# A graph layer on one core: half of the second messages behind the first factors, loads of h, gate weights and x re-timed, two last sums on GpSimd

## The chip, the cores and the metric

The kernel runs on one core of a Trainium2 chip. The metric is the device time of one launch in microseconds. The kernel before takes 1845.73 us, the median of three runs from 1843.53 to 1846.13 us. The profile was taken in a run of its own, whose span is 1848.1 us.

A core has five engines with instruction streams of their own: TensorE (PE in the profile; its weight loads are PEld), VectorE (DVE), ScalarE (ACT), GpSimd (POOL) and SyncE (SP). SP, ACT and GpSimd also issue transfers (DMA) between the memory outside the core and the core's own memory. "L597" is line 597 of the kernel before.

## The reference

There are 32 batches of 512 tokens with 256 channels. Each batch is normalised over its channels and cut at zero (h). From h come a convolution of 17 taps along the tokens, a message passing whose weights are distances between tokens, and a gate cell (a GRU step) that joins both.

```python
h = jnp.maximum(_layernorm(x, axis=-1), 0.0)
x = x + _L0_gnn_ref(h, adj, ...)

# _L0_gnn_ref, cut; here x is h and mask is adj
xc = jnp.transpose(x, (0, 2, 1))
h = _bn(_conv1d(xc, conv1_w, 0), ...)              # 1 tap
h = jax.nn.relu(h)
h = _bn(_conv1d(h, conv2_w, 8), ...)               # 17 taps
x_conv = jnp.transpose(jax.nn.relu(h + xc), (0, 2, 1))
s = x @ w_se.T + b_se                              # 3 numbers for each token
sq = jnp.sum(s * s, axis=-1)
dist = sq[:, :, None] + sq[:, None, :] - 2.0 * jnp.einsum('bnd,bmd->bnm', s, s)
A = jnp.exp(-dist) * mask
msg = jax.nn.relu(x @ w_msg.T + b_msg)
x_nmp = jnp.einsum('bnm,bmd->bnd', A, msg)
gi = jnp.concatenate([x_conv, x_nmp], axis=-1) @ w_ih.T + b_ih
gh = x @ w_hh.T + b_hh
r = jax.nn.sigmoid(gi_r + gh_r)
z = jax.nn.sigmoid(gi_z + gh_z)
nn_ = jnp.tanh(gi_n + r * gh_n)
return (1.0 - z) * nn_ + z * x
```

## The kernel before

The kernel works in three stages. The first two are done for half of the batches (16, called a group g) and then for the other half.

1. `first_part`: load x, normalise it, transpose it (h), do the convolution of 1 tap (`conv1`) and turn windows of its result into frequencies (`windows_to_freq`). For the second group GpSimd also builds sums of gate weights in this stage (`combine_weights`), one per turn of the loop over batches.
2. `nodes`: messages, distances and their product for each batch; between them stand the products of the 17-tap convolution in frequencies (`product`, tile `y`).
3. The gates for pairs of batches: the convolution's way back (`inverse`), `gates_rz`, `gate_n`, and `last_z` for the last pair.

The steps that the change touches, cut:

```python
def load_x(b, queue=nc.sync):
    X[b] = ... tile([P, NC, D], FP, tag="x", bufs=3)      # 512 KB
    queue.dma_start(X[b], x[b].rearrange("(c p) d -> p c d", p=P))

def statistics(b):
    for c in range(NC):
        nc.vector.bn_stats(stats[:, c, :], X[b][:, c, :])             # L285
    for c in range(NC):
        nc.vector.bn_aggr(mv[:, c, :], stats[:, c, :])                # L287
    ...
    nc.vector.tensor_scalar(rstd, mv[:, :, 1], LN_EPS, None, op0=ALU.add)            # L290
    nc.gpsimd.tensor_tensor(rstd, rstd, minus_half[:, :NC], op=ALU.pow)              # L291

# normalise(b): xn = (x - mean) * rstd on VectorE (L304)
# transpose_h(b): 8 transposes of xn on TensorE (phT), max with 0 on VectorE into hT (L316), hT stored to HD[b]
# conv1(b): 16 matmuls (pc), bias on VectorE (L331), relu on ACT

# first_part, the loop over the batches of a group (the turn of b0 itself cut):
for b in range(b0, b1):
    if b + 3 < b1:
        load_x(b + 3, nc.gpsimd)
    ...
    if b + 2 < b1:
        statistics(b + 2)
    if b + 1 < b1:
        transpose_h(b + 1)
    if b + 2 < b1:
        normalise(b + 2)
    one, two = between(b - b0)       # second group: one step of combine_weights
    if b > b0 + (g == 0):
        conv1(b)
    ...
    for step in one:
        step()
    windows_to_freq(b - 1, xf)

# combine_weights: for each of three weight matrices one load into a tile w (one buffer for w4),
# then four steps with one sum on GpSimd each (L886), and a store of the sums
if k == 0:
    steps.append([])
steps[-1].append(load)
...
    steps.append([partial(nc.gpsimd.tensor_tensor, q[dst], x1, x2, op=op)])

# by_chunks(b): ACT copies HT[b], in another order, to HQ[b] (L425)
def message(b):
    hq = HQ.pop(b)
    for c0 in range(0, NC, h):                     # two halves of two chunks
        for j in range(h):
            # 2 accumulating matmuls into a bank pm (L439), bias on VectorE: st (L441), msg (L442)
        nc.scalar.activation(m, m, AF.Relu)        # L443
# features(b): VectorE writes fl and fr from st
# factors(b): TensorE transposes fl (psl) and fr (psr), ACT copies them to sl (L460) and sr (L465)
# affinity(b): 4 matmuls pd of sl and sr (L474), exp on ACT, times adj on VectorE: A
# aggregate(b): matmuls pn of msg and A (L489), copied by ACT

# nodes(g, ...):
load_adj(todo[0])
begin(0)                                           # message and features of todo[0]
message(todo[1])
factors(todo[0])
features(todo[1])
affinity(todo[0])
for i, b in enumerate(todo):
    ...
    if i + 2 < GB and todo[i + 2] not in HT:
        load_h(todo[i + 2])                        # HD[b] back into hT, on the SP queue
    if more:
        load_adj(todo[i + 1])
        factors(todo[i + 1])
    ...                                            # a product, aggregate in parts
    begin(i + 2)                                   # by_chunks, message, features
    if more:
        affinity(todo[i + 1])
    ...

# last_z, the end of the kernel:
# turned(i, j): multiply and transpose on VectorE into o; added(i, j): xb += o on VectorE (L673)
turned(1, 0)
gated(b3, u3, 1, 1)                                # VectorE addition, sigmoid on ACT
nc.vector.tensor_add(u2, u2, b3)
added(1, 0)
store(p, 0, [nc.sync, nc.scalar])                  # four transfers, in turn on two queues
into(b5[0], ...); gated(b5[0], u2, 0, 1, ts[0])
turned(1, 1)
into(b5[1], ...); gated(b5[1], u2, 0, 1, ts[1])
added(1, 1)
for t in ts:
    turned(0, 1, t); added(0, 1, t); store(p, 1, [nc.sync, nc.scalar], t)
```

Of the kernel before, what the change touches and what calls it, by code (L numbers as in the profile page):

```python
# [11 lines left out]
FP = mybir.dt.float32  # L12
AF = mybir.ActivationFunctionType
ALU = mybir.AluOpType

P = 128
# [49 lines left out]
def gnn_layer(  # L66
# [15 lines left out]
    nc = tc.nc  # L82
    B, N, D = x.shape
    KT = w2T.shape[1]
    PAD = KT // 2
    NS = w_seT.shape[1]
# [338 lines left out]
            nc.scalar.copy(chunks(HQ[b][:, ic, :]), by_chunk(HT[b][:, ic, :]))  # L425
        del HT[b]

    def message(b):
        MSG[b] = pools["nodes"].tile([P, NC, D], FP, tag="msg", name=f"msg_{b}", bufs=3)
        ST[b] = pools["nodes"].tile([P, 2, NC, NS], FP, tag="st", name=f"st_{b}", bufs=2)  # L430
        hq = HQ.pop(b)
        h = N // D
        for c0 in range(0, NC, h):
            m = MSG[b][:, c0 : c0 + h, :]
            for j in range(h):
                c = c0 + j
                p = bank(f"pm_{b}_{c}")
                for ic in range(DC):
                    nc.tensor.matmul(p[:, : D + NS], hq[:, ic, c * P : (c + 1) * P], wmsg[:, ic, :],  # L439
                                     start=(ic == 0), stop=(ic == DC - 1))  # L440
                nc.vector.tensor_add(ST[b][:, 0, c, :], p[:, D : D + NS], bmsg[:, D:])  # L441
                nc.vector.tensor_add(m[:, j, :], p[:, :D], bmsg[:, :D])  # L442
            nc.scalar.activation(m, m, AF.Relu)  # L443

    def features(b):

# [62 lines left out]
    def combine_weights():  # L509

        steps = []
        for k, src in enumerate((w_hhT, w_ihT[D:], w_ihT[:D])):
            w, t = (pools["sums"].tile([P, n, 3 * P], FP, tag=f"w{n}", name=f"w{n}_{k}", bufs=m) for n, m in ((4, 1), (7, 2)))
            rows = w.rearrange("p (c h) m -> p c (h m)", c=DC)
            load = (partial(nc.sync.dma_start, rows, src.rearrange("(c p) m -> p c m", p=P)) if k == 1 else
                    partial(load_rows, rows, src, nc.sync))
            if k == 0:
                steps.append([])
            steps[-1].append(load)

            a11, a21, a12, a22 = (
                w[:, 2 * c : 2 * c + 2].rearrange("p h m -> p (h m)").rearrange("p (g i o) -> p g i o", i=2, o=32)[:, :, i]
                for c in range(DC) for i in range(2)
            )
            q = [t[:, n].rearrange("p (g o) -> p g o", o=32) for n in range(7)]
            for (dst, x1, x2, op), kept in zip(
                ((Q5, a21, a22, ALU.add), (Q6, q[Q5], a11, ALU.subtract),
                 (Q7, a11, a21, ALU.subtract), (Q3, a12, q[Q6], ALU.subtract)),
                ((Q1, a11), (Q2, a12), (Q4, a22), None),
            ):  # L530
                steps.append([partial(nc.gpsimd.tensor_tensor, q[dst], x1, x2, op=op)])
                if kept:
                    steps[-1].append(partial(nc.scalar.copy, q[kept[0]], kept[1]))
            steps[-1].append(partial(nc.sync.dma_start, WS[k], t.rearrange("p q (g o) -> p q g o", o=P)))
        return steps
# [58 lines left out]
    def into(bk, q, o, ks, terms, first, t=slice(0, N)):  # L594

        for i, k in enumerate(ks):
            nc.tensor.matmul(bk[:, t], sw[:, k, q, o, :], terms[k][q][:, t], start=(first and i == 0), stop=(i == len(ks) - 1),  # L597
                             skip_group_check=True)
# [50 lines left out]
    def last_z(p, terms):  # L649

        d, o, ks = RZ[p], 1, range(K3)

        def gated(src, other, i, j, t=slice(0, N)):
            z, g = d[:, DC + i, j, t], DC + i
            if other is not None:
                nc.vector.tensor_add(z, other[:, t], src[:, t])
                src = z
            nc.scalar.activation(z, src, AF.Sigmoid, bias=brz[:, g : g + 1], scale=1.0)

        def places(i, t):  # L660
            return slice(t.start // 32, t.stop // 32), slice(32 * i, 32 * (i + 1))

        def turned(i, j, t=slice(0, N)):
            dst, (js, half) = d[:, i, j, t], places(i, t)
            nc.vector.tensor_mul(dst, dst, d[:, DC + i, j, t])
            if (p, j) not in OUT:
                OUT[p, j] = pools["late"].tile([P, N // 32, D // 4], FP, tag="o", name=f"o_{p}_{j}", bufs=2)
            nc.vector.transpose(OUT[p, j][:, js, half], dst.rearrange("p (j k) -> p j k", k=32))

        def added(i, j, t=slice(0, N)):  # L670
            js, half = places(i, t)
            x = XP[p][j][:, js, half]
            nc.vector.tensor_add(x, x, OUT[p, j][:, js, half])  # L673

        b1, b2, b3, b4, *b5 = (bank(f"pz{k}_{p}") for k in range(1, 7))
        into(b1, Q1, o, ks, terms, True)
        p1 = temp("p1", f"z{p}")
        nc.scalar.copy(p1, b1)
        into(b2, Q6, o, ks, terms, True)
        u2 = temp("u2", f"z{p}")  # L680
        nc.vector.tensor_add(u2, p1, b2)
        into(b1, Q2, o, ks, terms, False)
        gated(b1, None, 0, 0)
        early_out(p, 1, 1)
        turned(0, 0)
        into(b2, Q7, o, ks, terms, False)
        u3 = temp("u3", f"z{p}")
        nc.vector.tensor_add(u3, p1, b2)
        early_out(p, 0, 1)
        added(0, 0)  # L690
        into(b4, Q4, o, ks, terms, True)
        gated(b4, u3, 1, 0)
        into(b3, Q5, o, ks, terms, True)
        turned(1, 0)
        gated(b3, u3, 1, 1)
        nc.vector.tensor_add(u2, u2, b3)
        added(1, 0)
        store(p, 0, [nc.sync, nc.scalar])

        ts = [slice(h * N // 2, (h + 1) * N // 2) for h in range(2)]  # L700
        into(b5[0], Q3, o, ks, terms, True, ts[0])
        gated(b5[0], u2, 0, 1, ts[0])
        turned(1, 1)
        into(b5[1], Q3, o, ks, terms, True, ts[1])
        gated(b5[1], u2, 0, 1, ts[1])
        added(1, 1)
        for t in ts:
            turned(0, 1, t)
            added(0, 1, t)
            store(p, 1, [nc.sync, nc.scalar], t)  # L710
# [90 lines left out]
    def store(p, j, queues, t=slice(0, N)):  # L801
        js = slice(t.start // 32, t.stop // 32)
        for g in range(4):
            queues[g % len(queues)].dma_start(quarter(out[2 * p + j], g)[:, js], XP[p][j][32 * g : 32 * (g + 1), js])
# [6 lines left out]
    def first_part(g, freq, between, left=()):  # L811
# [37 lines left out]
        normalise(b0 + 1, g > 0)  # L849
        fill()  # L850
        for b in range(b0, b1):
            if b + 3 < b1:
                load_x(b + 3, nc.gpsimd)
            if b == b0:
                conv1(b)
                one, two = between(0) if g == 0 else ([], [])
                for step in one:
                    step()
                fill()
                if g == 0:  # L860
# [3 lines that stand above are left out]
                else:  # L864
                    normalise(b + 2)
                    transpose_h(b + 1)
                fill()
                xf, last_two = freq(g), two
                continue
            if g == 0 and b == b0 + 1:  # L870
                conv1(b)
                for step in last_two:
                    step()
            if b + 2 < b1:
                statistics(b + 2)
            if b + 1 < b1:
                transpose_h(b + 1)
            if b + 2 < b1:
                normalise(b + 2)
            one, two = between(b - b0)  # L880
            if b > b0 + (g == 0):
                conv1(b)
            if b == b1 - 1:
                load_h(b0)
# [3 lines that stand above are left out]
            for step in two:  # L888
                step()
# [13 lines left out]
    with tc.tile_pool(name="freq", bufs=1) as fpool:  # L903
# [29 lines left out]
        def nodes(g, xf, units, last):  # L933
# [11 lines left out]
            load_adj(todo[0])  # L945
            with tc.manual_schedule():
                begin(0)
                message(todo[1])
                factors(todo[0])
                features(todo[1])  # L950
            affinity(todo[0])
            for i, b in enumerate(todo):
# [4 lines left out]
                    load_x(b1)  # L957
                if g + 1 < NG and i == 3 * GB // 4:
                    statistics(b1)
                if i + 2 < GB and todo[i + 2] not in HT:  # L960
                    load_h(todo[i + 2])
                if more:
                    load_adj(todo[i + 1])
                    factors(todo[i + 1])
# [4 lines left out]
                for u in mine[:1]:  # L969
                    product(pools["pw"], g, u, xf)  # L970
                begin(i + 2)
                if more:
                    affinity(todo[i + 1])
                for u in mine[1:2]:
# [109 lines left out]
```

## Time and profile before

| What | us |
|---|---|
| median of the runs | 1845.73 |
| span of the profile | 1848.1 |
| first part, first group | about 0 to 165 |
| nodes, first group | about 165 to 467 |
| first part, second group | about 467 to 580 |
| nodes, second group | about 580 to 880 |
| gates | about 880 to 1848 |
| TensorE busy | 1826.4 |
| VectorE, GpSimd, ACT busy | 1109.1, 588.2, 581.9 |

The limits of the stages are read from the chain of work that ended last, where the lines of one stage give way to those of the next.

How to read the answers of the profile that are shown below. A line of the view of waits names the engine, the tile and line that waited, what it waited for, and then the total in us, how often, and the longest. A line of the order of time gives the start in us, the length in us of the piece, engine, line and operation, the tile written and the tiles read, their shapes, the number of instructions merged, and in brackets the idle time before it and what ended that. A line of the view of windows gives the window, its length, the busy time of TensorE, of its weight loads, of VectorE, ACT and GpSimd (each with a count of instructions), then the granted clock of TensorE (1.00 is full), the share of the DMA engines, and GB/s.

### The profile page before, as it was taken

Reading aid. Unit: us, or ns where it says so; the run is one execution under the profiler, and the core shown is the slowest. Engines: PE = TensorE matmul, PEld = TensorE weight load, DVE = VectorE, ACT = ScalarE, POOL = GpSimd, SP = SyncE. Lnnn points to the kernel's source line nnn. Section 1 sums busy time; section 2 is a strip of 40 time slices with the busy share of each in tenths; the row PEclk is TensorE's granted clock in tenths of the full one; section 3 lists DMA queues with packets and bytes.
Section 4 is the critical chain, followed back from the end, with each engine's and each line's share of the span. In section 5 each row is a group of like instructions: output and inputs, shape, how many; then the busy total and the mean of one; then the engine's idle time right before and its main releaser. Section 6 shows DMA issues by size and latency. Waiting matters only on the chain.

```text
span 1848.1 us, 20105 instructions
## 1 busy us (share of the span) xinstructions
PE 1826.4 (99%) x6610; PEld 1089.0 (59%) x6610; DVE 1109.1 (60%) x2220; ACT 581.9 (31%) x1083; POOL 588.2 (32%) x572
## 2 busy tenths in 40 slices
PE   9999999999999999999999999999999999999998
PEld 6777666666888666665555554555455544555443
DVE  7775656554885555545266466655666466645666
ACT  4555434432335333333222221222122221222121
POOL 3331333333432344444422323133212322133221
PEclk9999999999999999999999999999999999999999
DMA  8999888875678887778421443234422442244312
GB/s 233 299 276 241 225 226 246 218 179 180 212 250 207 235 245 235 216 207 261 123 86 34 120 120 99 53 88 120 120 78 43 120 120 88 49 103 120 112 25 52
DMA packets 307452, 289.26 MB, mean 157 GB/s; under 512 B 148028, under 2 KB 237148, under 8 KB 306964
## 3 DMA queue, kind: packets, MB, share of 16 engines
q1 hardware_dynamic: 281300, 224.22, 46.0%
q10 hardware_dynamic: 19024, 38.68, 5.9%
q0 software_dynamic: 7024, 25.07, 4.8%
q8 instruction: 53, 0.87, 0.2%
q14 instruction: 51, 0.42, 0.1%
HBM read 191.50 MB, written 96.40 MB: 156 GB/s over the span
## 4 chain that ended last, share of the span: by engine, by line
PE 89%; DVE 4%; issue 3%; DMA 2%; POOL 1%; ACT 1%; SPq 0%; POOLq 0%; ACTq 0%; DVEq 0%
PE pg L597 29%; PE pn L597 14%; PE pn L489 11%; PE py L393 11%; PE pm L439 6%; PE pc L585 5%; PE pc L328 3%; PE px L343 3%; PE pw L256 2%; PE pd L474 2%; PE phT L312 1%; DMA w<-in_w_ihT_dram 1%; PE psr L463 1%; DVE stats L285 1%; DVE xn L304 1%
## 5 line engine op out<-in xcount | busy, mean ns | idle before, releaser
L489 PE MATMUL pn<-A,msg 128*128 128x512 f32 x512 | 225.9, 593 | 0.6 <-DVE A L480 0.6
L597 PE MATMUL pg<-hp,sw 128*128 128x512 f32 x434 | 221.8, 593 | 0.7 <-DVE rz L616 0.5
L597 PE MATMUL pg<-np,sw 128*128 128x512 f32 x434 | 221.6, 592 | 0.0
L597 PE MATMUL pg<-cp,sw 128*128 128x512 f32 x434 | 221.6, 592 | 0.0
L575 POOL TENSOR_TENSOR hp<-hp 128x512 f32<-128x512 f32 x64 | 81.3, 1280 | 413.0 <-DMA hp<-hd 234.6
L372 POOL TENSOR_TENSOR both<-xf 128x256 f32<-128x256 f32 x78 | 60.1, 771 | 329.1 <-PE py L393 297.5
L489 PEld LDWEIGHTS pn<-A,msg 128*128 128x128 f32 x512 | 97.2, 191 | 110.9 <-issue 105.7
L575 POOL TENSOR_TENSOR cp<-cp 128x512 f32<-128x512 f32 x64 | 80.4, 1267 | 229.8 <-ACT cp L591 228.6
L393 PE MATMUL py<-wt,both 128*128 128x256 f32 x624 | 151.0, 385 | 0.7 <-issue 0.7
L612 ACT ACTIVATE rz<-rz,brz 128x512 f32<-128x512 f32 x93 | 67.0, 721 | 260.2 <-DVE rz L616 260.2
L400 DVE TENSOR_TENSOR y<-y,py 128x256 f32<-128x256 f32 x78 | 31.8, 408 | 190.5 <-ACT y L399 185.8
L597 PEld LDWEIGHTS pg<-hp,sw 128*128 128x128 f32 x434 | 82.2, 190 | 104.8 <-issue 97.8
L597 PEld LDWEIGHTS pg<-cp,sw 128*128 128x128 f32 x434 | 82.5, 190 | 103.8 <-issue 103.8
L597 PEld LDWEIGHTS pg<-np,sw 128*128 128x128 f32 x434 | 82.5, 190 | 103.8 <-issue 103.8
L393 PEld LDWEIGHTS py<-wt,both 128*128 128x128 f32 x624 | 114.3, 190 | 43.2 <-issue 28.3
L480 DVE TENSOR_TENSOR A<-e,at 128x512 f32<-128x512 f32 x128 | 114.5, 933 | 36.9 <-ACT e L477 36.7
L359 POOL TENSOR_TENSOR wsum<-wt 128x512 f32<-128x512 f32 x78 | 109.1, 1399 | 51.8 <-DMA wt<-wd 39.1
L735 ACT ACTIVATE nt<-nt,vech 128x512 f32<-128x512 f32 x64 | 46.2, 722 | 235.8 <-DVE nt L734 235.8
L328 PE MATMUL pc<-w,hT 128*128 128x256 f32 x512 | 116.7, 381 | 1.6 <-DVE hT L316 1.6
L439 PE MATMUL pm<-wmsg,hq 128*128 128x259 f32 x512 | 117.5, 382 | 0.6 <-ACT sl L460 0.6
L597 PE MATMUL pn<-np,sw 128*128 128x512 f32 x224 | 114.4, 592 | 0.0
L597 PE MATMUL pn<-cp,sw 128*128 128x512 f32 x224 | 114.4, 592 | 0.0
(146 smaller groups left out, 2963.6 us busy)
## 6 DMA issues: line engine op xcount, KB each, us to landing
wt<-wd SPq DMA_DIRECT2D x160, 256.0 KB, 4.3
adj<-in_adj_dram SPq DMA_DIRECT2D x128, 256.0 KB, 5.4
wd<-wst SPq DMA_DIRECT2D x64, 320.0 KB, 5.3
yd<-y ACTq DMA_DIRECT2D x80, 256.0 KB, 4.3
yt<-yd SPq DMA_DIRECT2D x30, 640.0 KB, 7.5
hd<-hT SPq DMA_DIRECT2D x32, 512.0 KB, 4.4
nd<-nmp ACTq DMA_DIRECT2D x32, 512.0 KB, 4.0
xb<-in_x_dram SPq DMA_DIRECT2D x128, 128.0 KB, 3.8
```

The source lines that it names most:

```text
L328: nc.tensor.matmul(p[:, j, :], HT[b][:, ic, c * P : (c + 1) * P], w1[:, ic, :], start=(ic == 0), stop=(ic == DC - 1))
L343: nc.tensor.matmul(p[:, j * 2 * L : (j + 1) * 2 * L], H1[b][:, c0 + j, ic * P : (ic + 1) * P], fwd, start=True, stop=True)
L359: nc.gpsimd.tensor_tensor(t, WT[g, u][:, 0], WT[g, u][:, 1], op=ALU.add)
L372: nc.gpsimd.tensor_tensor(both[:, 0], re, im, op=ALU.add)
L393: nc.tensor.matmul(dst, v[:, ic, :], w[:, ic, :], start=(ic == 0), stop=(ic == DC - 1))
L439: nc.tensor.matmul(p[:, : D + NS], hq[:, ic, c * P : (c + 1) * P], wmsg[:, ic, :], start=(ic == 0), stop=(ic == DC - 1))
L480: nc.vector.tensor_mul(A[b][:, mc, :], e, at)
L489: nc.tensor.matmul(p, MSG[b][:, mc, dc * P : (dc + 1) * P], A[b][:, mc, :], start=(mc == 0), stop=(mc == NC - 1))
L575: nc.gpsimd.tensor_tensor(t[:, dst, :], t[:, a, :], t[:, b, :], op=sub)
L585: nc.tensor.matmul(bk[:, t0:t1], YT[p][j][:, c, oc * P : (oc + 1) * P], back[:, n : n + t1 - t0], start=(c == 0), stop=(c == len(spans) - ...
L597: nc.tensor.matmul(bk[:, t], sw[:, k, q, o, :], terms[k][q][:, t], start=(first and i == 0), stop=(i == len(ks) - 1), skip_group_check=True)
L612: nc.scalar.activation(rz[:, g, j, :], src, AF.Sigmoid, bias=brz[:, g : g + 1], scale=1.0)
```

## The change

Five things are moved; no computation is added or left out.

- In `nodes` the second half of the message of the second batch goes behind the factors of the first batch, so that TensorE has matmuls to do while ACT copies the factors.
- The load of h for a batch is asked for one step sooner: three batches ahead behind `begin(i + 2)`, in place of two batches ahead at the head of the next turn.
- Gate weights: an empty step is put between the load of the second and third matrix and their first sum, so the load has one turn of the loop more.
- In the first part of the second group the load of x three batches ahead, on GpSimd's queue, moves from the head of the turn to behind the statistics of the batch two ahead, whose last operation, the power, is done by GpSimd.
- In `last_z` two additions go from VectorE to GpSimd, one of them earlier in the order, and the four stores of the first batch of the pair all go to the SP queue.

```diff
-    def message(b):
+    def message(b, halves=range(2)):
...
-        for c0 in range(0, NC, h):
+        for c0 in (h * k for k in halves):
...
@@ combine_weights
             steps[-1].append(load)
+            if k > 0:
+                steps.append([])
@@ last_z
-        added(1, 0)
-        store(p, 0, [nc.sync, nc.scalar])
+        added(1, 0, engine=nc.gpsimd)
+        store(p, 0, [nc.sync])
...
         turned(1, 1)
+        added(1, 1, engine=nc.gpsimd)
         into(b5[1], Q3, o, ks, terms, True, ts[1])
         gated(b5[1], u2, 0, 1, ts[1])
-        added(1, 1)
@@ first_part
-            if b + 3 < b1:
+            if b + 3 < b1 and (g == 0 or b == b0):
                 load_x(b + 3, nc.gpsimd)
...
             if b + 2 < b1:
                 statistics(b + 2)
+            if g > 0 and b > b0 and b + 3 < b1:
+                load_x(b + 3, nc.gpsimd)
@@ nodes
-                message(todo[1])
+                message(todo[1], [0])
                 factors(todo[0])
+                message(todo[1], [1])
                 features(todo[1])
...
-                if i + 2 < GB and todo[i + 2] not in HT:
-                    load_h(todo[i + 2])
...
                 begin(i + 2)
+                if i + 3 < GB:
+                    load_h(todo[i + 3])
```

More of the change, by code (lines that the diff above doesn't have):

```diff
@@ L426, in by_chunks @@
         del HT[b]
-    def message(b):
[L429 to L432, printed above, removed]
-        for c0 in range(0, NC, h):
+    def message(b, halves=range(2)):
+        if 0 in halves:
+            MSG[b] = pools["nodes"].tile([P, NC, D], FP, tag="msg", name=f"msg_{b}", bufs=3)
+            ST[b] = pools["nodes"].tile([P, 2, NC, NS], FP, tag="st", name=f"st_{b}", bufs=2)
+        hq = HQ[b]
+        h = NC // 2
+        for c0 in (h * k for k in halves):
             m = MSG[b][:, c0 : c0 + h, :]
@@ L443, in message @@
             nc.scalar.activation(m, m, AF.Relu)
+        if 1 in halves:
+            del HQ[b]
     def features(b):
@@ L661, in places, with turned @@
             return slice(t.start // 32, t.stop // 32), slice(32 * i, 32 * (i + 1))
-        def turned(i, j, t=slice(0, N)):
+        def turned(i, j, t=slice(0, N), engine=nc.vector):
             dst, (js, half) = d[:, i, j, t], places(i, t)
-            nc.vector.tensor_mul(dst, dst, d[:, DC + i, j, t])
+            engine.tensor_tensor(dst, dst, d[:, DC + i, j, t], op=ALU.mult)
             if (p, j) not in OUT:
@@ L668, in turned, with added @@
             nc.vector.transpose(OUT[p, j][:, js, half], dst.rearrange("p (j k) -> p j k", k=32))
-        def added(i, j, t=slice(0, N)):
+        def added(i, j, t=slice(0, N), engine=nc.vector):
             js, half = places(i, t)
             x = XP[p][j][:, js, half]
-            nc.vector.tensor_add(x, x, OUT[p, j][:, js, half])
+            engine.tensor_tensor(x, x, OUT[p, j][:, js, half], op=ALU.add)
         b1, b2, b3, b4, *b5 = (bank(f"pz{k}_{p}") for k in range(1, 7))
```

## The prediction

> **What bounds the kernel now.** I began with the first part of the page, the busy shares.
>
> ```profile
> PE 1826.4 (99%) x6610; PEld 1089.0 (59%) x6610; DVE 1109.1 (60%) x2220; ACT 581.9 (31%) x1083; POOL 588.2 (32%) x572
> ```
>
> TensorE is busy for 1826.4 of 1848.1 us. The change takes no matmul away, so everything that it can win lies in the other 21.7 us, and in matmuls that run slowly. A gain over 2% (36.9 us) isn't to be had; a loss has no such limit. So I asked next for whom TensorE waits.
>
> ```profile
> PE pd L474 <- ACT sr L465: 2.7, 2, 1.3
> PE row L824 <- DVE fr L224: 1.9, 1, 1.9
> PE pc L328 <- DVE hT L316: 1.6, 2, 1.1
> PE pd L474 <- DVE y L400: 1.5, 1, 1.5
> PE phT L312 <- DVE xn L304: 1.4, 1, 1.4
> ```
>
> Three of these five lines are aims of the change. The distances `pd` wait twice for the copied factor `sr` (at 173.3 and at 587.3 us, once in each half). They wait once for `y` (at 219.5 us), and one transpose of x waits for the normalised rows (at 550.0 us). The windows around them show a second price:
>
> ```profile
> 172.00:176.00 4.00, 2.66 (x18) 1.52 (x17) 2.51 (x9) 1.68 (x5) 1.34 (x2) 1.00 1.15 268
> 176.00:179.40 3.40, 3.40 (x12) 2.93 (x12) 0.00 (x0) 1.66 (x4) 1.19 (x1) 0.50 1.25 198
> ...
> 223.80:227.20 3.40, 3.40 (x9) 2.49 (x8) 3.08 (x6) 2.34 (x5) 1.97 (x3) 0.50 0.94 325
> ...
> 586.00:590.00 4.00, 2.66 (x18) 1.52 (x17) 2.19 (x11) 1.66 (x5) 0.00 (x0) 1.00 1.25 183
> ```
>
> The third figure from the end is the granted clock. After the waits at 173 and 219 us it is 0.50 for 3.4 us each; after the one at 587 us it stays 1.00.
>
> The last view is the order of time on GpSimd and VectorE in the first part of the second half (465 to 580 us), because the diff also moves a load of x there that the headline doesn't name.
>
> ```profile
> 500.52 1.03 POOL L291 TENSOR_TENSOR rstd<-rstd,minus_half 128x4 f32<-128x4 f32 x1 [3.57 <-DVE rstd L290]
> 501.53 0.98 POOL L886 TENSOR_TENSOR w<-w 128x384 f32<-128x384 f32 x1
> 502.47 0.84 POOL L118 DMA_DIRECT2D x<-in_x_dram  x1
> 506.86 1.03 POOL L291 TENSOR_TENSOR rstd<-rstd,minus_half 128x4 f32<-128x4 f32 x1 [3.56 <-DVE rstd L290]
> ```
>
> ```profile
> 504.83 1.39 DVE L285 BATCH_NORM_STATS2 stats<-x 128x6 f32<-128x256 f32 x4
> 506.15 0.35 DVE L287 BATCH_NORM_AGGREGATE mv<-stats 128x2 f32<-128x6 f32 x4
> 506.54 0.17 DVE L290 TENSOR_SCALAR rstd<-mv 128x4 f32<-128x4 f32 x1
> ```
>
> One batch goes by every 6.3 to 6.5 us here. GpSimd issues a load of x as the last thing of a turn, and then idles 3.6 us until VectorE has the next statistics: the load goes out ahead of that wait.
>
> **What the skill says.** The Trainium skill, "TensorE: Matmul & The Clock Gate", Part 1, says that the clock falls to 4/8 after an idle window of some 3.4 us and comes back after a busy one, with windows that run freely; its terms give the penalty as the slow time times (1 - K/N). The trace agrees in the size (0.50 for 3.4 us) and in the chance (same wait at 587 us, no fall), though the waits themselves were only 1.3 and 1.5 us. The same Part 1 says that GpSimd takes its instructions strictly first in, first out, and "DMA: Bandwidth & Descriptors", Anatomy of one DMA, that a semaphore wait happens on the issuing sequencer ahead of the DMA. Together: a load behind a waiting instruction on GpSimd waits too. The trace agrees at 492.4 us, where a sum of gate weights waited 4.5 us for its DMA and the load of x behind it went out at 493.3 us. The same DMA page gives about 2.0 us plus bytes at 436 GB/s, which would be 3.2 us for 512 KB (an estimate from that page). The trace shows more, 4.4 us at the least in this stage, and I use that.
>
> **Part 1, half of the second messages behind the first factors.** Before, TensorE ends `psr`, waits for ACT to copy `sl` and `sr`, and idles 1.34 us. After, four chunks' worth of message matmuls are split, and two chunks stand between `psr` and `pd`. Eight chunks took 7.12 us on the chain, so two take 1.78 us, more than 1.34. Both waits go: 2 x 1.34 = 2.7 us. The slow window after the first (3.4 us at half clock) costs 3.4 x 0.5 = 1.7 us, and I count it as gone. Sum: -4.4 us.
>
> **Part 2, h one step sooner.** At 219.5 us the chain runs: `y` goes out at 208.64, lands 214.18, only then the SP queue issues the load of `hT` (214.24, landing 219.07), ACT stands in its copy `hq` until then, and its copy of `y`, which frees a bank, comes behind. After, this load stands ahead of the second pair of `wt` loads and no longer behind them and the landing of `y`. Going by when those went out (four from 202 to 208 us) it leaves near 204 and lands near 209 us, before ACT asks at 213. The wait (1.5) and its slow window (1.7) go: -3.2 us. Two small waits near 597 and 635 us (0.7 and 0.6) may go or stay; I take half of them: -0.6.
>
> **Part 3, gate weights one step sooner.** GpSimd waited 4.7 and 6.5 us for `in_w_ihT`. With one empty step in between, that wait has 6.5 us more and is all but gone. Before, it delayed the `rstd` behind it and so cost the 1.45 us at 550 us, and about 2 us more in turns of 6.9 to 7.3 us in place of 6.5. This would be worth about -3.3 us, if nothing else set the turn.
>
> **Part 4, the load of x behind the power.** But something else will. In the new order GpSimd does `rstd` of batch b+2 and then issues x of b+3, and the next turn opens with the statistics of b+3. That closes a ring: x lands; VectorE does statistics, aggregate and `rstd` (546.77 - 544.88 = 1.9 us where it was seen to start on a landing); GpSimd does the power (0.1 to start, 1.03); the load is issued; it lands. The thirteen loads of this stage took 4.5, 4.4, 8.8, 5.2, 5.4, 4.8, 9.0, 5.2, 6.9, 4.5, 9.4, 4.9 and 4.5 us from issue to landing. The 8.8, 9.0 and 9.4 ran beside gate weights; the median of the other ten is 4.85. So a turn takes 1.9 + 0.1 + 1.0 + 4.9 = 7.9 to 8.0 us, against 6.5 of TensorE's work. Before, the same load had 504.83 - 496.10 = 8.7 us until its use; now it has about 3.5, less than the shortest landing seen.
>
> Carried through the stage: twelve loads (x of batches 20 to 31) come in the ring. The first goes out after the power at 481.24, so at 482.25, beside the weights of `w_hhT`, where a load took 8.8: it lands at 491.05. Eleven turns of 7.95 follow, 87.5 us, and the other two weight loads, each with a write of 1344 KB, add some 3 us each (half to three quarters of the 4 us excess seen, for they now start a little after x). The last statistics then start at 491.05 + 87.5 + 6 = 584.5, against 559.67 before: +24.8. TensorE stands waiting at that point and gets through the rest of the stage (0.87 + 3.46 + 2.17 + 3.46 + 4.35 = 14.3 us, begun some 4 us after the statistics) in 18.5 us, where before it took 19.9: -1.4. The stage costs +23.4 us, and the gains of part 3 drown in it. TensorE will idle 1.5 us per turn, so the clock may fall at times; slow matmuls would fill idle time first, and I add nothing.
>
> **Part 5, the end.** Two additions of 0.6 us each leave VectorE's last chain, and two stores leave ACT's queue, which held back a sigmoid by 0.7 us (ready at 1839.04, begun 1839.73, ACT issuing from 1838.74). On the other side GpSimd needs about 1.3 us for such an operation, the last addition must wait for it, and one queue issues four stores. I take -0.8.
>
> **Sum.** 1845.7 - 4.4 - 3.2 - 0.6 + 23.4 - 0.8 = 1860.1 us.
>
> **Rivals.** First: the loads of x come in time, and the change does what its headline says. For it: the DMA engines are loaded less if turns grow longer, and GpSimd no longer waits for weights. Against: even 4.4 us, the shortest landing, makes the ring 7.4. The time would be 1845.7 - 4.4 - 3.2 - 0.6 - 3.3 - 0.8, about 1833. Second: the ring holds, but the x, `hd` and weight transfers collide as badly as 9 us each time, because `hd` is now written at the same moment as x is read. That makes the turn 12 us and the time about 1905; the loads at 496.1 and 502.5 us, near which `hd` was written, took only 5.4 and 4.8. Third: the ring is as I say and the gains in parts 1 and 2 don't come, as another operation takes the bank or the clock falls elsewhere: about 1868.
>
> **Range and chances.** A ring of 7.4 without weight collisions would cost about 13 us (to 1850); one of 8.3 with full collisions about 30 (to 1867). With uncertain gains of 3 us on either side I take 1846 to 1870, and 1860 in the middle. Over 2% either way needs under 1808.8, which idle TensorE doesn't have, or over 1882.6, which needs the second rival: 0.01 and 0.04. I give the first rival about one in ten, and it too is within 2%.
>
> **What would show it.** In the profile after: from about 480 us on VectorE's statistics wait for the DMA of x in nearly every turn, 1 to 2 us each; turns of about 8 us; GpSimd's `rstd` starts 2 us after each landing and the load right behind it; TensorE waits there for `hT` or `xn`, some 20 us in all. The waits of `pd` for `sr` are gone, and so is the one at 219 us with its slow clock. If statistics do not wait for x, part 4 is wrong and with it the sign; if turns are over 10 us, its landing time is.

## The result and the profile after

The changed kernel takes 1867.39 us (median, from 1865.42 to 1869.87 us) against 1844.93 us for the kernel before beside it: the ratio is 1.0123, with a 95% interval of 1.0105 to 1.014. It is slower by 1.2%. The prediction was 1860, with a range of 1846 to 1870.

The busy shares of the profile after, from its page:

```profile
PE 1834.4 (98%) x6610; PEld 1092.6 (58%) x6610; DVE 1116.5 (60%) x2218; ACT 582.2 (31%) x1083; POOL 590.8 (32%) x574
```

The same 6610 matmuls now fill 1834.4 of 1868.1 us, so TensorE idles 12 us more and is 8 us slower while busy. Whom it waits for, in the view of waits:

```profile
PE phT L312 <- DVE xn L304: 14.8, 6, 5.2
PE row L829 <- DVE fr L224: 1.9, 1, 1.9
PE py L393 <- DMA wt<-wd: 1.4, 1, 1.4
...
PE pm L440 <- ACT hq L425: 1.0, 1, 1.0
```

The waits of `pd` for `sr` and for `y` are gone. In their place stand 14.8 us in which the transposes wait for normalised rows, and two new waits in the nodes stage (`py` for its weights, `pm` for `hq`). What VectorE waited for in the first part of the second group (476 to 585 us) is one line:

```profile
DVE stats L285 <- DMA x<-in_x_dram: 24.1, 12, 5.5
```

All twelve statistics of the ring wait for their x; before, three did:

```profile
DVE stats L285 <- DMA x<-in_x_dram: 2.9, 3, 1.4
```

The turn itself, in the order of time on GpSimd and then on VectorE:

```profile
496.06 1.03 POOL L291 TENSOR_TENSOR rstd<-rstd,minus_half 128x4 f32<-128x4 f32 x1 [5.49 <-DVE rstd L290]
497.06 0.79 POOL L118 DMA_DIRECT2D x<-in_x_dram  x1
497.87 1.01 POOL L893 TENSOR_TENSOR w<-w,w 128x384 f32<-128x384 f32 x1
504.22 1.02 POOL L291 TENSOR_TENSOR rstd<-rstd,minus_half 128x4 f32<-128x4 f32 x1 [5.34 <-DVE rstd L290]
```

```profile
494.03 1.41 DVE L285 BATCH_NORM_STATS2 stats<-x 128x6 f32<-128x256 f32 x4 [1.13 <-DMA x<-in_x_dram]
495.36 0.36 DVE L287 BATCH_NORM_AGGREGATE mv<-stats 128x2 f32<-128x6 f32 x4
495.75 0.17 DVE L290 TENSOR_SCALAR rstd<-mv 128x4 f32<-128x4 f32 x1
495.83 1.29 DVE L316 TENSOR_SCALAR hT<-phT 128x512 f32<-128x512 f32 x2
497.13 2.89 DVE L304 TENSOR_SCALAR xn<-x,mv,rstd 128x256 f32<-128x256 f32 x4
499.93 1.28 DVE L331 TENSOR_TENSOR h<-pc,shift_row 128x512 f32<-128x512 f32 x2
502.26 1.41 DVE L285 BATCH_NORM_STATS2 stats<-x 128x6 f32<-128x256 f32 x4 [1.05 <-DMA x<-in_x_dram]
```

Follow it round: x lands at 494.03, the power starts at 496.06, the load goes out at 497.06, x lands at 502.26, and the next power starts at 504.22. The turn is 8.16 us. GpSimd idles over 5 us in it and still issues late, since the load stands behind the power.

The stages of both profiles, cut at the first matmul of each (the second first part begins with its first `pc`, the gates with the first `pc` of `inverse`):

| Stage | before, us | after, us | difference | predicted |
|---|---|---|---|---|
| first part, first group | 165.5 | 163.8 | -1.7 | 0 |
| nodes, first group | 301.6 | 298.6 | -3.0 | -6.2 |
| first part, second group | 112.4 | 138.3 | +25.9 | +23.4 |
| nodes, second group | 302.3 | 299.7 | -2.6 | -1.9 |
| gates, to the last matmul | 957.3 | 957.2 | 0 | 0 |
| last matmul to the end | 9.0 | 10.5 | +1.5 | -0.8 |

### The profile page after: what moved, and what is told of

Its sections match the earlier page's. It is cut to its first block, busy times and chain, and to the rows that moved or that the text cites. A ratio compares the mean times of both kernels' runs of the same rounds, so it can differ in the third digit from the quotient of the medians.

```text
span 1868.1 us, 20100 instructions
## 1 busy us (share of the span) xinstructions
PE 1834.4 (98%) x6610; PEld 1092.6 (58%) x6610; DVE 1116.5 (60%) x2218; ACT 582.2 (31%) x1083; POOL 590.8 (32%) x574
## 4 chain that ended last, share of the span: by engine, by line
PE 63%; issue 2%; DVE 1%; POOL 1%; DMA 0%; ACT 0%; SPq 0%; POOLq 0%; DVEq 0%; ACTq 0%
PE pg L602 29%; PE pn L602 14%; PE pn L492 6%; PE py L393 6%; PE pc L590 5%; PE pm L440 2%; PE pd L477 1%; PE psr L466 0%; DVE A L483 0%; POOL cp L580 0%; POOL nt L792 0%; POOL rz L791 0%; DMA out_dram<-xb 0%; POOL xb L787 0%; DVE at L482 0%
## 5 line engine op out<-in xcount | busy, mean ns | idle before, releaser
L372 POOL TENSOR_TENSOR both<-xf 128x256 f32<-128x256 f32 x78 | 60.6, 777 | 326.6 <-PE py L393 289.4
L328 PE MATMUL pc<-w,hT 128*128 128x256 f32 x512 | 123.0, 396 | 1.4 <-DVE hT L316 1.4
L602 PE MATMUL pn<-hp,sw 128*128 128x512 f32 x224 | 114.4, 592 | 0.0
```

The source lines that it names most:

```text
L328: nc.tensor.matmul(p[:, j, :], HT[b][:, ic, c * P : (c + 1) * P], w1[:, ic, :], start=(ic == 0), stop=(ic == DC - 1))
L372: nc.gpsimd.tensor_tensor(both[:, 0], re, im, op=ALU.add)
```

## The experiments

All ratios are to the kernel before, run beside each; a ratio need not be the quotient of two medians. Executions of one variant spread over up to 13 us, those of the kernel before over 13 to 18, so differences of 1 to 3 us between variants are near the limit of what these runs can tell.

**The load of x early, all else changed (x_early).**

```diff
-            if b + 3 < b1 and (g == 0 or b == b0):
+            if b + 3 < b1:
                 load_x(b + 3, nc.gpsimd)
...
-            if g > 0 and b > b0 and b + 3 < b1:
-                load_x(b + 3, nc.gpsimd)
```

> The changed kernel with only the load of x put back to the head of the turn; messages, h, gate weights and the end stay changed. Ring theory (load behind the power, power behind the statistics, statistics behind the landing): the twelve waits of the statistics for x vanish, a turn is 6.5 us again, the first part of the second group takes some 25 us less: about 1841 us, below the kernel before. Rival, the loss comes from another part (order of h, gate weights, the end): stays near 1867 us.

Measured: 1840.49 us, ratio 0.9973 (0.9962 to 0.9983). The first part of the second group takes 109.4 us. Its waits of VectorE (470 to 560 us):

```profile
DVE stats L285 <- DMA x<-in_x_dram: 2.6, 2, 2.4
```

Twelve waits became two, the two that collide with gate weights. With this one move undone the change is faster than the kernel before. The order on GpSimd is that of before again, load first and then the idle time:

```profile
496.47 0.99 POOL L891 TENSOR_TENSOR w<-w 128x384 f32<-128x384 f32 x1
497.42 0.84 POOL L118 DMA_DIRECT2D x<-in_x_dram  x1
501.81 1.03 POOL L291 TENSOR_TENSOR rstd<-rstd,minus_half 128x4 f32<-128x4 f32 x1 [3.56 <-DVE rstd L290]
```

**The load of x late, nothing else (x_late_alone).** The kernel before with the reverse of the edit above.

> The kernel before with only the load of x moved behind the power; nothing else changed. Ring theory: turns of 8 us and more, some 25 us more from the first to the last statistics of the stage, about 1868 to 1872 us. Rival, the loss needs the other moved loads: near 1845 us.

Measured: 1869.12 us, ratio 1.0129 (1.0111 to 1.0148); statistics wait 23.0 us in twelve places, and the stage takes 136.0 us. The one move makes the whole loss; the rest of the change isn't needed for it.

**The same place in the program, another queue (x_sync_queue).**

```diff
             if g > 0 and b > b0 and b + 3 < b1:
-                load_x(b + 3, nc.gpsimd)
+                load_x(b + 3, nc.sync)
```

> The changed kernel with the load of x at the same place of the program, but on the SP queue, which does not wait for the power. Ring theory: the load goes out behind the store of h of the turn before, well ahead of the statistics; the waits shrink to under 1 us or vanish, about 1841 to 1846 us. Rival, the place in time or the collision of x with the store of h on the DMA engines is what costs: remains above 1858 us.

Measured: 1843.93 us, ratio 0.9982 (0.9972 to 0.9992), the stage 114.0 us. On a queue that doesn't wait for the power, the same line of the program costs 3.4 us over x_early and not 27: the place in the program isn't the cause, the order behind the power is. What is left is 8.4 us of waits in four places; the loads in flight beside a load of gate weights, now on the same queue, took 7.2 to 9.6 us to land, the others 4.4 to 6.8.

**One useless operation in the ring (x_late_plus_op).** `slow` is a tile of its own that nobody reads.

```diff
             if g > 0 and b > b0 and b + 3 < b1:
+                nc.gpsimd.tensor_tensor(slow, STATS[b + 2][1], minus_half[:, :NC], op=ALU.pow)
                 load_x(b + 3, nc.gpsimd)
```

> The changed kernel with a second, useless power of the same 128x4 size (1.03 us) on GpSimd between the power and the load of x, in the twelve turns. Ring theory: this operation lies in the ring, so each turn grows by 1.0 us, 12 us in all: about 1879 us. Rival, the turn is set by how fast the DMA engines move x, h and gate weights: GpSimd idles 5 us per turn and the time stays within 2 us of the changed kernel, 1867.

Measured: 1873.34 us, ratio 1.0151 (1.0134 to 1.0168). That is 6 us over the changed kernel: half of what the ring theory expected, and more than its rival. The order of time shows where the other half went in one turn:

```profile
497.86 1.03 POOL L292 TENSOR_TENSOR rstd<-rstd,minus_half 128x4 f32<-128x4 f32 x1 [4.37 <-DVE rstd L291]
498.96 1.06 POOL L883 TENSOR_TENSOR slow<-rstd,minus_half 128x4 f32<-128x4 f32 x1
499.93 0.79 POOL L118 DMA_DIRECT2D x<-in_x_dram  x1
506.06 1.03 POOL L292 TENSOR_TENSOR rstd<-rstd,minus_half 128x4 f32<-128x4 f32 x1 [4.29 <-DVE rstd L291]
```

```profile
498.92 1.39 DVE L305 TENSOR_SCALAR xn<-x,mv,rstd 128x256 f32<-128x256 f32 x4
...
504.09 1.40 DVE L286 BATCH_NORM_STATS2 stats<-x 128x6 f32<-128x256 f32 x4 [2.59 <-DMA x<-in_x_dram]
```

The load goes out 1.1 us later in its turn, but lands 4.1 us after its issue and no longer 5.2, so this turn is 8.2 us, as without the extra operation. In the changed kernel x goes out in the same moment as the store of `hd` (whose `hT` is written up to 497.1); here it follows about 1 us behind. That this store is what made the landing longer fits the times, but wasn't tried by itself. The normalisation `xn` also takes 1.39 us here and 2.89 there.

**Three of them (x_late_plus_3_ops).** The same line in a loop of three.

> As x_late_plus_op, with three useless powers in place of one. One added 6 us in all where 12 were expected, and the landing of x was 4.1 to 4.3 us in place of 5.2 in the turns without gate weights, as the load then came behind the store of h. Ring theory with this collision: no more of the landing can be saved, so each of the two further operations adds 1.1 us in each of twelve turns, 26 us: about 1899 us. Rival, the turn is set by the DMA engines: under 1885 us.

Measured: 1894.94 us, ratio 1.0258 (1.023 to 1.0285). The turns are 10.6 to 11.2 us now. From the first power of the ring to the last, twelve turns take 105.6 us in the changed kernel, 110.0 with one operation and 130.3 with three. The three parts of the ring, added up over the twelve turns of each profile, account for it:

| Part, us in twelve turns | changed kernel | one operation | three operations |
|---|---|---|---|
| power to the issue of the load | 12.6 | 25.4 | 52.7 |
| issue to landing | 68.4 | 60.6 | 53.7 |
| landing to the next power | 24.6 | 23.9 | 23.9 |

Of the 27.3 us that the last two operations put in, 6.9 came back in shorter landings; my expectation that no more of the landing could be saved was wrong, and that is why 20 us came and not 26. A limit of the DMA engines alone would not have grown by this. The turn is the ring; whatever x collides with on its way is inside the landing time.

**The end as before (x_early_old_end).** x early, both additions on VectorE, four stores on two queues.

```diff
-        added(1, 0, engine=nc.gpsimd)
-        store(p, 0, [nc.sync])
+        added(1, 0)
+        store(p, 0, [nc.sync, nc.scalar])
...
-        added(1, 1, engine=nc.gpsimd)
         into(b5[1], Q3, o, ks, terms, True, ts[1])
         gated(b5[1], u2, 0, 1, ts[1])
+        added(1, 1)
```

> The changed kernel with the load of x at the head of the turn and the end as before (both additions on VectorE, four stores on two queues); messages, h and gate weights stay changed. The profiles of the changed kernel and of x_early show 10.5 and 10.8 us from the last matmul to the end, the kernel before 9.0. Theory, the end of the change loses: 9.0 us again, so about 1.5 us less than x_early, 1839 us. Rival, the end as predicted gains 0.8 us: about 1841 us and a longer end.

Measured: 1837.82 us, ratio 0.9951 (0.9933 to 0.9969), and 9.0 us from the last matmul to the end against 10.8 in x_early. The end of the change loses 1.8 us by the profiles. (The medians differ by 2.7 us, with intervals that overlap.) This is the best version found: all but the two moves that lose.

**Half of the end (x_early_half_end).** As before at the end, and h as before too (next experiment), but `added(1, 0)` on GpSimd and its four stores on SP.

> As x_early_old_end_old_h, but of the end's changes one is kept: the addition for the first batch of the pair on GpSimd and its four stores on the SP queue; the second addition is on VectorE, at its old place. Theory, the loss at the end comes from the second addition on GpSimd, which holds up VectorE's product (1.45 in place of 0.42 us) and its next addition: the end is 9.0 us or shorter, perhaps 8.4. Rival, it comes from the six to eight stores on one queue: 10 us or more.

Measured: 1843.93 us, ratio 0.9981 (0.9969 to 0.9993), and 9.1 us for the end. So the longer end goes away with the second addition; the first wins nothing either. The end of the changed kernel on VectorE:

```profile
1858.73 1.45 DVE L670 TENSOR_TENSOR rz<-rz 128x256 f32<-128x256 f32 x1
1860.21 0.45 DVE L673 STREAM_TRANSPOSE o<-rz 128x256 f32<-128x256 f32 x1
1861.10 0.42 DVE L678 TENSOR_TENSOR xb<-xb,o 128x256 f32<-128x256 f32 x1 [0.44 <-DMA out_dram<-xb]
```

and on GpSimd at that time:

```profile
1858.64 1.25 POOL L678 TENSOR_TENSOR xb<-xb,o 128x512 f32<-128x512 f32 x1 [1.84 <-DVE o L673]
```

The same product in x_early_half_end, where GpSimd doesn't add beside it:

```profile
1835.54 0.41 DVE L670 TENSOR_TENSOR rz<-rz 128x256 f32<-128x256 f32 x1
```

VectorE's product takes 1.45 us instead of 0.41 as long as GpSimd adds; that is 1.0 us on the last chain, more than the 0.6 us of the addition that was taken off it. The next addition then waits 0.44 us. The chain had begun 0.4 us earlier, so the last addition ends 5.2 us after the last matmul and not 4.75. That is 0.45 of the 1.5 us. Most of the rest is a wait on the SP queue, seen in the view of waits of the changed kernel (1857 to 1868 us) and at no store of the end before:

```profile
SPq L809 <- DMA out_dram<-xb: 2.0, 1, 2.0
```

Here SP stands until a store that ACT issued has landed (6.3 us after the last matmul), and only then issues the last three stores, 1.1 us after the last addition. The wait is there in x_early_half_end too (1.5 us). There the last addition ends 0.4 us earlier than before, but SP's last two stores go out 1.1 and 1.6 us behind it, and the gain is lost. So both halves of the change cost something: the second addition holds up VectorE, and with the first addition and its four stores on SP comes the wait. Which of these last two brings it wasn't tried.

The median of 1843.93 lies 3.1 us above the version with the whole old end and h as before, with overlapping intervals and the same 9 us of end: the end doesn't explain that. The two profiles differ by 5.3 us, of which 3.4 us are the price of two more stretches at half clock ahead of 230 us, where the edit changes nothing. Why the medians differ stays open.

**h as before (x_early_old_end_old_h, then again as best_old_h beside best_again).**

```diff
+                if i + 2 < GB and todo[i + 2] not in HT:
+                    load_h(todo[i + 2])
...
-                if i + 3 < GB:
-                    load_h(todo[i + 3])
```

> As x_early_old_end, with the load of h also back to two batches ahead at the head of the turn; only the messages and the gate weights stay changed. Theory, h one step sooner gives nothing on average: the wait of 0.98 us of the message for hq near 195 us, there in three of three profiles with the sooner h, goes, and the wait near 219 us comes back in some executions; within 2 us of x_early_old_end, 1837 to 1841. Rival, h sooner is worth the predicted 3.2 us: about 1842 us.

> x_early_old_end once more (x at the head of the turn, old end; messages, h and gate weights changed), as the base for the three beside it: about 1838 us, some 0.4 to 0.5% below the kernel before.

> x_early_old_end_old_h once more: the base with h asked for as before. The first measurement put it 3 us above x_early_old_end with touching intervals. Theory, h one step sooner is worth about what was predicted (3.2 us on average): 1841 us again. Rival, executions scatter: equal to the base within 1 us.

Measured: 1840.86 us (0.997, 0.9955 to 0.9984) and 1841.31 us (0.9972, 0.9961 to 0.9982), against 1837.82 and, again, 1838.96 us (0.9955, 0.9939 to 0.9971) with h sooner. Twice the sooner h is 2.4 to 3.0 us better, near the predicted 3.2, though the intervals of each pair overlap. (The mean of all 36 runs with the old h is 1841.3 us, of the 14 with the sooner h 1838.1.) One reason is seen in the windows of best_old_h:

```profile
216.00:218.30 2.30, 1.72 (x8) 0.59 (x4) 1.62 (x8) 0.65 (x2) 0.00 (x0) 1.00 1.25 189
218.30:225.10 6.80, 6.80 (x15) 4.54 (x14) 5.63 (x16) 3.80 (x7) 2.20 (x3) 0.50 0.79 217
```

A wait of 0.58 us (in the first window) is followed by 6.8 us at half clock, a price of 3.4 us. Of the five profiles with the old h, three have such a stretch near 220 us; of the nine with the sooner h, none has one there, and only the changed kernel has one nearby, at 200.5 us. My expectation in the first of these, that the wait for `hq` near 195 us goes with the sooner h, was wrong: it is there with the old h too, and only gone when the messages are in one piece (below).

**Gate weights as before (best_old_gate_weights).**

```diff
-            if k > 0:
-                steps.append([])
```

> The base with the empty step taken out: the second and third matrix of gate weights are asked for one step before their first sum. Theory, the empty step saves the waits of GpSimd for them: the first part of the second group takes about 112.4 us as in the kernel before in place of 109.0 to 109.4, about 3 us more in all. Rival, the place of the load of x covers it: equal within 1 us.

Measured: 1840.29 us, ratio 0.9966 (0.9952 to 0.998), 1.3 us over the base (best_again), which the intervals don't separate. By the profiles the stage takes 111.0 us against 109.7, and a wait of 1.0 us for `xn` at 544 us is back. The empty step is worth less than the expected 3 us when x is early: 1.3 us by the medians, and by the profiles little more than their scatter, since the seven with x early and the empty step have 109.0 to 110.6 us for this stage.

**Messages as before (best_old_messages).**

```diff
-                message(todo[1], [0])
+                message(todo[1])
                 factors(todo[0])
-                message(todo[1], [1])
```

> The base with the second message in one piece ahead of the factors. Theory: pd waits 1.34 us for sr again in both groups, against new waits of 0.4 (psl) and 1.0 us (message for hq) that go in the first group, and a slow clock of 3.4 us in some executions: 1 to 4 us more. Rival, the two new waits take back all: equal within 1 us.

Measured: 1840.38 us, ratio 0.9963 (0.9951 to 0.9974), 1.4 us over the base; again the intervals overlap. The profile shows the mechanism, in its waits of TensorE:

```profile
PE pd L477 <- ACT sr L468: 2.7, 2, 1.3
```

Both waits are back, each followed by a slow clock of 3.4 us here (from 174.9 and 584.5 us). What the split gives in its place is smaller: in best_again 0.9 us for `psl`, 1.0 us for `hq`, and 0.6 us that are left of the wait for `sr`.

## Why the prediction was right, and where it wasn't

**Part 4, the ring: right, and shown.** It was named before any run, from the order of instructions and the landings before. Undoing the move takes some 27 us away (1867.39 to 1840.49, measured at different times), doing it alone adds 21.9 (1847.26 to 1869.12), another queue frees it, and operations put into it lengthen it by what they take, less what the landings save. From power to power over twelve turns I had 481.24 to 586.5, 105.3 us; the profile has 476.46 to 582.08, 105.6 us. Two terms in it were off and cancelled: the landing was 5.3 us (median of the last eleven) and not 4.9, most likely because x now leaves together with the store of h; and the later gate weights cost less, 0.4 to 1.3 us a landing (5.7 to 6.6 us, four of them), where I had 6 us in all. I also had TensorE waiting some 20 us in the ring and statistics 1 to 2 us each; it was 14.8 us, and 0.9 to 5.5 us. The remainder of the stage was mis-sized: I gave TensorE 18.5 us from the last statistics to the nodes stage, it took 20.6. One step that failed there is "slow matmuls would fill idle time first, and I add nothing". The windows of the changed kernel, with the clock as the third figure from the end:

```profile
490.60:494.00 3.40, 3.12 (x11) 2.61 (x12) 2.30 (x6) 1.60 (x4) 0.00 (x0) 0.50 0.57 200
...
535.00:538.40 3.40, 3.40 (x9) 2.70 (x8) 2.33 (x11) 2.39 (x7) 0.31 (x1) 0.50 0.10 37
...
575.90:582.80 6.90, 6.02 (x18) 4.88 (x19) 5.62 (x17) 2.93 (x7) 1.30 (x2) 0.51 0.39 132
```

The last of them reaches 2.8 us past the last statistics, where TensorE no longer has idle time to spare: at half clock, up to 1.4 us. The rest is the 18.5 us itself, which was too small: x_late_alone, with no slow clock after its last statistics, took 19.4.

**Parts 1 and 2, messages and h: right mechanism, too large for this profile.** Both waits of `pd` for `sr` and the one at 219 us went. But the first group gained 3.0 us and not 6.2, for two waits came in their place, which I hadn't looked for (TensorE, from 189 us):

```profile
194.09 3.77 PE L440 MATMUL pm<-wmsg,hq 128*128 128x259 f32 x16 [0.98 <-ACT hq L425]
...
200.37 3.65 PE L393 MATMUL py<-wt,both 128*128 128x256 f32 x8 [1.43 <-DMA wt<-wd]
```

The second of them, for the weights that now stand behind h on the queue, was followed by a slow clock of its own; it was this large in no other version. Also, the slow window after a wait isn't a fixed term: the profile of x_late_alone, which has the old order of messages and h, has the wait of 1.34 us at 172 us, no slow clock there and no wait near 219. Executions differ by this, so a single profile of before can overstate what such a wait costs on average.

**Part 3, gate weights: right in sign, too large.** The stage goes from 112.4 to 109.4 us with x early (-3.3 predicted). But 111.0 us in best_old_gate_weights, which has the same program in this stage as the kernel before, suggests that about half of this is scatter; the empty step alone is some 1.3 us. In the changed kernel it drowned in the ring, as said.

**Part 5, the end: wrong in sign.** The step that failed is the count of two additions taken off VectorE. I gave GpSimd's addition 1.3 us and had it beside VectorE's work. It isn't beside it: VectorE's product of two operands in the core's own memory ran 1.0 us longer while it lasted. The Trainium skill, "SBUF — State Buffer", Who interferes with whom, states that a VectorE instruction with two such inputs contends with a GpSimd instruction that reads there, and I should have drawn on it; this trace agrees, 1.45 against 0.41 us. The first addition did leave VectorE's chain with a gain, 0.4 us in x_early_half_end. The sigmoid is no longer held back either, but nothing waited for it. And I counted the stores that leave ACT's queue as a gain, and missed that SP's last stores would wait for one of ACT's, some 1 us at the end.

By stage the profile lies off the prediction by -1.7 (a shorter slow clock at the start, which is chance), +3.2, +2.5, -0.7 and +2.3 us. That is 5.6 us, the distance between the predicted and the profiled difference (14.4 and 20.0 us). So 1867 against 1860 is a right ring with smaller gains around it.

## What to carry to other kernels

In these traces GpSimd, which both computes and issues loads, issued each load only when it had done the operation ahead of it: a load put behind an operation that needs the data of the load before it closes a ring, whose turn is computing time plus landing time (8.2 us here, of which the landing is 5.2), however idle the engines are. Look in the instruction order for what a moved load now stands behind, and compare its distance to its use with the shortest landing in the trace. Where TensorE is 99% busy, a wait of 1 us can cost less than the slow clock that may follow it (1.7 us for 3.4 us at half clock), and whether one follows differs from execution to execution.

## What the runs showed of the hardware that was not expected

- Half clock follows waits much shorter than the 3.4 us that most of its stretches last: after 0.58 us of wait it lasted 6.8 us (best_old_h), while after 1.34 us (x_late_alone) it didn't come at all.
- A load of 512 KB issued in the same moment as a store of 512 KB landed in 5.2 us, and in 4.1 us when issued 1 us later, so a delay of 1.1 us at its issue cost that turn nothing (the turns shown above; over all turns the landings with the delay took 4.1 to 7.8 us).
- Four normalisations on VectorE take 1.4 us alone, 1.5 while GpSimd issues a load (after, at 522.09 us), 2.1 while it does a sum of gate weights (x_sync_queue, at 485.10 us), 2.1 with the sum first and the issue behind it (before, at 501.58 us), and 2.9 with the issue first and the sum behind it (after, at 497.13 us). The order of two small operations on GpSimd costs VectorE 0.8 us.
- A store issued by SP waited for the landing of a store issued by ACT (2.0 us in the changed kernel), so in this program the two queues weren't independent at the end.
